# The last image's depthwise filter: the third channel tile on ScalarE and GpSimd, two sums in PSUM

## The chip, the cores and the metric

The kernel runs on one core of one Trainium2 chip. The metric is the device time of one execution in microseconds (us). The engines are named as in the profile: PE (TensorE, matrix products), PEld (its weight loads), DVE (VectorE), ACT (ScalarE), POOL (GpSimd) and SP (SyncE, which issues DMAs). Each engine runs its instructions in the order in which they were queued, and waits at an instruction whose inputs or buffers are not ready.

## The reference

The input `x` has 8 images of 384 channels and 64 x 64 points, all float32. Two layers follow each other. The first is `x + attention(group_norm(x))`, linear attention with six heads. The second, to which the change belongs, is

```python
t = jnp.einsum('bchw,oc->bohw', x, w_in)             # x is group-normalised
tp = t.reshape(b, hid, hb, P, wb, P)                 # 8 x 8 patches
tf = jnp.fft.rfft2(tp, axes=(3, 5))
tf = tf * fft_filter[None, :, None, :, None, :]
t = jnp.fft.irfft2(tf, s=(P, P), axes=(3, 5)).reshape(b, hid, h, w)
t = jax.lax.conv_general_dilated(t, w_dw, ..., feature_group_count=hid)   # 3 x 3, each channel alone
x1, x2 = (t[:, :hid // 2], t[:, hid // 2:])
g = jax.nn.gelu(x1, approximate=False) * x2
return jnp.einsum('bchw,oc->bohw', g, w_out)
```

and its result is added to the layer's input. The change moves part of the 3 x 3 filter, in which every channel has nine weights ("taps") of its own.

## The kernel before, in words

An image's 64 rows are cut into eight bands of 8 rows (512 points), and its 384 channels into three tiles of 128 partitions. The second layer takes one band at a time:

- `normalised` (L364 to L375): ACT writes the normalised band `hf`, three instructions.
- `expand_filter` (L745 to L774): PE makes `pi` in four quarters of 128 points, each a PSUM tile; ACT copies each to `ht`; PE turns `ht` into the patches' frequencies `pd`; DVE multiplies by the filter into `tf`.
- `back_transform` (L776 to L804): PE transforms back into `pb`; ACT copies that into a ring of two buffers that hold ten rows each, the band's eight and one edge row on either side. L801 copies the upper edge row from the band before, and L802 gives the band before its lower edge row. So a band's last three taps, which read its lower row, can run only once the next band is in the ring.
- `first_taps` (L839 to L846): ACT writes the first tap of each tile into the sums `dw`.
- `taps` and `tile_taps` (L848 to L860): DVE adds the other eight taps of each tile, one instruction each, `sum = ring * weight + sum` (L854), on 128 x 512 elements.
- `gate_taps` (L862 to L871): ACT takes the gelu of tile 0 (L866), and DVE multiplies it by tile 1 (L867). Tile 2 is gated with itself, half by half: two gelus on ACT (L870) and two products on DVE (L871). The result is `gated`.
- `contraction` (L877 to L917): PE multiplies `gated` by `w_out` into four PSUM tiles `pw`; ACT copies them to `y` (L912), and a DMA that POOL issues adds `y` to the output in memory (L917). For the very last band DVE adds instead (L914), and SP writes.

For the first seven images, the next image's first layer runs between these steps and fills PE. The last image has nothing to put between, and its second layer is a loop of its own at the end of the kernel (L1226 to L1246). In its last two bands PE filters the third tile with diagonal matrices (`on_array`, `array_taps`, PSUM tile `ptap`).

The order in which a scheduler queues the instructions on each engine is fixed when the kernel is built, by priority and by what each instruction needs. All PSUM tiles come from one pool of eight buffers, one per bank: `pi`, `pd`, `pb`, `pw` and `ptap` share them, and a tile waits for a buffer until the readers of its last holder are done. Work tiles in SBUF (`hf`, `ht`, `tf` and others) come from a pool of nine buffers (`w_tile`).

Of the kernel before, what the change touches and what calls it, by code (L numbers as in the profile page):

```python
# [9 lines left out]
F32 = mybir.dt.float32  # L10
BF16 = mybir.dt.bfloat16
AF = mybir.ActivationFunctionType
ALU = mybir.AluOpType

P = 128
C = 384
CT = 3
# [3 lines left out]
BT = N // NBAND  # L21
# [96 lines left out]
def conv_blocks_kernel(ctx: ExitStack, tc: tile.TileContext, a: dict, out: bass.AP, nb: int):  # L118
    nc = tc.nc
# [4 lines left out]
    taps_pool = ctx.enter_context(tc.tile_pool(name="taps", bufs=2))  # L124
# [5 lines left out]
    def ps_tile(name):  # L130
        return psum.tile([P, 512], F32, tag="ps", name=name)

    def w_tile(shape, name):
        return work.tile(shape, F32, tag="w", name=name)
# [98 lines left out]
    def const_tile(shape, name, src, queue=nc.scalar):  # L233
        t = const.tile(shape, F32, tag=name, name=name)
        queue.dma_start(t, src)
        return t
# [14 lines left out]
    scale = HD ** -0.5  # L251
# [9 lines left out]
    ring = []  # L261
# [543 lines left out]

    dw, dw_pe, diagonals = {}, {}, []

    def on_array(b, j):

        return b == nb - 1 and j >= NBAND - 2  # L810
# [7 lines left out]
    def array_taps(b, j, ks):  # L818

        for k in ks:  # L820
            nc.tensor.matmul(
                dw_pe[b, j].rearrange("p (r w) -> p r w", w=W),
                diagonals[0][:, k * P : (k + 1) * P],
                ring[j % 2][:, 2, k // 3 : k // 3 + 8, k % 3 : k % 3 + W],
                start=(k == 0),
                stop=(k == 8),
            )
# [3 lines left out]
    def add_tap(b, j, k, m0):  # L831

        t = w_tile([P, CT, 8, W], f"tap_{b}_{j}_{k}")
        for m in range(m0, CT):
            nc.scalar.activation(t[:, m], ring[j % 2][:, m, 0:8, k : k + W], AF.Copy, scale=w_dw[:, m, k : k + 1])
            first_on_vector[b, j, m] = k + 1
        nc.gpsimd.dma_start(out=dw[b, j][:, m0:], in_=t[:, m0:], accum_op=ALU.add)

    def first_taps(b, j):  # L839

        acc = dw[b, j] = taps_pool.tile([P, CT, 8, W], F32, tag="dw", name=f"dw_{b}_{j}")
        for m in range(CT - on_array(b, j)):
            nc.scalar.activation(acc[:, m], ring[j % 2][:, m, 0:8, 0:W], AF.Copy, scale=w_dw[:, m, 0:1])
        if on_array(b, j):
            dw_pe[b, j] = ps_tile(f"ptap_{b}_{j}")
            array_taps(b, j, range(9 if j == NBAND - 1 else 6))  # L846

    def tile_taps(b, j, m, weights, ks=None):  # L848

        t, acc = ring[j % 2], dw[b, j]  # L850
        for k in ks or range(first_on_vector.pop((b, j, m), 1), 9):
            src = t[:, m, k // 3 : k // 3 + 8, k % 3 : k % 3 + W]
            wd = weights[:, m, k : k + 1]
            nc.vector.scalar_tensor_tensor(acc[:, m], src, wd, acc[:, m], ALU.mult, ALU.add)  # L854

    def taps(b, j):
        if on_array(b, j) and j < NBAND - 1:
            array_taps(b, j, range(6, 9))
        for m in range(CT - on_array(b, j)):
            tile_taps(b, j, m, w_dw)  # L860

    def gate_taps(b, j):  # L862
        g = gated
        af = dw.pop((b, j)).rearrange("p t r w -> p t (r w)")
        last = dw_pe.pop((b, j)) if on_array(b, j) else af[:, 2, :]
        nc.scalar.activation(g[:, :BT], af[:, 0, :], AF.Gelu)  # L866
        nc.vector.tensor_mul(g[:, :BT], g[:, :BT], af[:, 1, :])  # L867
        for h, gelu in enumerate((gelu2[64:P, :], g[64:P, BT:])):
            of = slice(h * HT, (h + 1) * HT)
            nc.scalar.activation(gelu, last[0:64, of], AF.Gelu)  # L870
            nc.vector.tensor_mul(g[halves[h], BT:], gelu, last[64:P, of])  # L871

    def depthwise_gate(b, j):
        taps(b, j)
        gate_taps(b, j)
# [218 lines left out]
    for c0, at, n in QRUNS:  # L1094

        t, p0, quarter, first = at // P, at % P, c0 // QC, c0 % QC
# [13 lines left out]
    w_dw = const_tile([P, CT, 9], "w_dw", a["w_dw"], nc.sync)  # L1110
# [30 lines left out]
    def last_band(b):  # L1141

        for k in (1, 2):
            add_tap(b, NBAND - 1, k, 1)
            yield

        ps = ps_tile(f"pwd_{b}")
        nc.tensor.matmul(
            ps[:, : CT * 9], ident, w_dw.rearrange("p t k -> p (t k)"), start=True, stop=True
        )  # L1150
        late_w = small.tile([P, CT, 9], F32, tag="late_w", name=f"late_w_{b}", bufs=1)
        nc.vector.tensor_copy(late_w, ps[:, : CT * 9].rearrange("p (t k) -> p t k", t=CT))
        yield
        for m in range(CT):
            if m == 0:
                tile_taps(b, NBAND - 1, m, w_dw, range(1, 8))
                tile_taps(b, NBAND - 1, m, late_w, range(8, 9))
            else:
                tile_taps(b, NBAND - 1, m, late_w)
            if m == CT - 1:  # L1160
                gate_taps(b, NBAND - 1)
            yield
        if b + 1 < nb - 1:
            contract(b, NBAND - 1)

    before_last, late = nothing, iter(())
    for b in range(nb):
# [4 lines left out]
        last = b == nb - 1  # L1172
# [14 lines left out]
        for j in range(NBAND):  # L1187
# [19 lines left out]
            some(2 * items)  # L1207
            back_transform(b, j, tf[0])
            first_taps(b, j)
            some(items)  # L1210
            if j > 1:
# [15 lines left out]
    b = nb - 1  # L1227
    h = ahead
    for j in range(NBAND):
        tf = []  # L1230
        layer1 = expand_filter(b, j, h, tf)
        run(layer1)
        store_x(b, j)
        if j < NBAND - 1:
            h = normalised(b, j + 1, params, (8, 8), "f")
        back_transform(b, j, tf[0])
        first_taps(b, j)
        if j >= 2:
            contract(b, j - 2)
        if j >= 1:  # L1240
            taps(b, j - 1)
            gate_taps(b, j - 1)
    contract(b, NBAND - 2)
    taps(b, NBAND - 1)
    gate_taps(b, NBAND - 1)
    contract(b, NBAND - 1)  # L1246
# [41 lines left out]
```

## Time and profile before

| | us |
|---|---|
| median of 3 runs | 3333.89 |
| lowest and highest | 3331.0, 3337.78 |
| profiled execution, its own time | 3330.32 |
| span of the profiled execution, first to last instruction | 3328.5 |
| PE busy | 3264.3 |
| DVE busy | 2752.7 |
| ACT busy | 2024.5 |
| POOL busy | 173.3 |
| DVE taps (L854), 1401 of them | 976.6 |
| first instruction of the last stage (`hf` of band 0), from the span's start | 3150.11 |
| first `pi` product of the last stage | 3150.98 |

Times inside the profile are counted from the start of the span. In a row of the timeline, the columns are the start, the duration (of a whole group where it ends in "x3" and the like), the engine, the source line, the operation, output and inputs with shapes, the count, and in brackets how long the engine stood idle before it and what ended that. In a row of a group of instructions, the part after the bar has the busy time in us, the mean of one in ns, and the idle time before with what ended it.

### The profile page before, as it was taken

The numbers are of one execution on the slowest core, as the hardware profiler recorded it, in microseconds if no ns is written. First come the engines' busy times: TensorE is split into PE (matmuls) and PEld (weight loads), VectorE is DVE, ScalarE is ACT, GpSimd is POOL, SyncE is SP. The second block draws the span as 40 slices with busy tenths as digits, with TensorE's granted clock in tenths as the row PEclk, the third lists the DMA queues.
The fourth block names the chain that finished last, engine by engine and source line by source line (L and its number), as shares of the span: only waits on it lengthen the run. The fifth ranks groups of instructions, "written<-read, shape, count | busy, mean of one in ns | idle before, by whom it ended". The sixth has DMA issues, their size and how long they took to land.

```text
span 3328.5 us, 53155 instructions
## 1 busy us (share of the span) xinstructions
PE 3264.3 (98%) x21133; PEld 1830.2 (55%) x21133; DVE 2752.7 (83%) x4528; ACT 2024.5 (61%) x4029; POOL 173.3 (5%) x321
## 2 busy tenths in 40 slices
PE   8999999999999999999999999999999999999988
PEld 5544566456654566545665456654566445664454
DVE  6577789977889688896888968988788987989698
ACT  4445666556666566655666656656576665556553
POOL 0000000100010000100001000010000100000000
PEclk9999999999999999999999999999999999999999
DMA  6334335352444423534335343454333541324113
GB/s 217 113 93 110 96 80 128 112 143 68 108 108 123 143 66 97 127 100 141 86 82 134 115 122 77 104 133 114 103 96 96 134 134 42 86 71 127 57 25 53
DMA packets 154445, 346.33 MB, mean 104 GB/s; under 512 B 29812, under 2 KB 41060, under 8 KB 146004
## 3 DMA queue, kind: packets, MB, share of 16 engines
q1 hardware_dynamic: 124500, 282.65, 26.0%
q0 software_dynamic: 29504, 60.06, 12.2%
q8 instruction: 166, 2.72, 0.3%
q14 instruction: 83, 0.68, 0.1%
q10 hardware_dynamic: 192, 0.21, 0.0%
HBM read 235.62 MB, written 99.93 MB: 101 GB/s over the span
## 4 chain that ended last, share of the span: by engine, by line
PE 73%; DVE 14%; issue 6%; ACT 4%; DMA 2%; POOL 0%; SPq 0%; DVEq 0%; POOLq 0%; ACTq 0%
PE pk L491 14%; PE pi L751 14%; PE pv L507 13%; PE pf L733 11%; PE pq L654 6%; DVE dw L854 5%; PE pw L887 3%; PE pb L786 2%; PE pd L765 2%; PE acc L523 2%; PE pw L898 2%; PE acc L536 2%; DVE qc L666 1%; DVE qs L666 1%; DMA wq<-in_wq 1%
## 5 line engine op out<-in xcount | busy, mean ns | idle before, releaser
L854 DVE SCALAR_TENSOR_TENSOR dw<-ring,w_dw,dw 128x512 f32<-128x512 f32 x1401 | 976.6, 745 | 240.1 <-ACT ring L802 201.1
L491 PE MATMUL pk<-wk,x 128*128 128x384 f32 x1536 | 544.0, 495 | 0.0
L654 PE MATMUL pq<-x,wq 128*128 128x512 f32 x1152 | 528.3, 606 | 2.6 <-ACT mt L570 2.6
L751 PE MATMUL pi<-w_in,hf 128*128 128x384 f32 x1536 | 514.1, 492 | 1.3 <-ACT hf L374 1.3
L733 PE MATMUL pf<-qc,mt 128*128 128x512 f32 x1152 | 510.7, 597 | 1.2 <-ACT y L912 1.2
L507 PE MATMUL pv<-wv,x 128*128 128x384 f32 x1344 | 470.0, 488 | 0.0
L751 PEld LDWEIGHTS pi<-w_in,hf 128*128 128x128 f32 x1536 | 288.2, 191 | 196.1 <-issue 3.1
L491 PEld LDWEIGHTS pk<-wk,x 128*128 128x128 f32 x1536 | 283.1, 190 | 204.8 <-issue 31.6
L514 ACT COPY v<-pv 128x384 f32<-128x384 f32 x224 | 108.6, 485 | 424.7 <-PE pv L507 423.4
L733 PEld LDWEIGHTS pf<-qc,mt 128*128 128x128 f32 x1152 | 214.3, 190 | 256.8 <-issue 243.1
L507 PEld LDWEIGHTS pv<-wv,x 128*128 128x128 f32 x1344 | 253.6, 190 | 181.4 <-issue 8.4
L654 PEld LDWEIGHTS pq<-x,wq 128*128 128x128 f32 x1152 | 213.7, 192 | 249.1 <-issue 232.8
L737 DVE SCALAR_TENSOR_TENSOR x<-pf,bfc,x 128x512 f32<-128x512 f32 x192 | 137.7, 739 | 84.2 <-PE pf L733 84.1
L379 ACT ACTIVATE qs<-qc 128x512 f32<-128x512 f32 (+1 forms) x128 | 106.9, 836 | 163.9 <-DVE qc L683 163.9
L180 ACT ACTIVATE differences<-x,shift 128x512 f32<-128x512 f32 x168 | 120.1, 715 | 113.1 <-DVE x L737 112.9
L887 PE MATMUL pw<-gated,w_out 128*128 128x256 f32 x768 | 179.8, 384 | 0.0
L494 DVE TENSOR_TENSOR kc<-pk,kvbias 128x384 f32<-128x384 f32 x256 | 140.3, 548 | 38.7 <-PE pk L491 38.7
L758 ACT COPY ht<-pi 128x384 f32<-128x384 f32 x256 | 115.0, 482 | 86.2 <-PE pi L751 82.3
L887 PEld LDWEIGHTS pw<-gated,w_out 128*128 128x128 f32 x768 | 146.8, 192 | 37.0 <-issue 7.9
L917 POOL DMA_DIRECT2D out_dram<-y x63 | 80.5, 1278 | 1591.7 <-DVE dw L854 830.0
L379 ACT ACTIVATE ks<-kc 128x1536 f32<-128x1536 f32 x64 | 95.0, 1485 | 94.9 <-DVE kc L498 94.1
L374 ACT ACTIVATE hf<-x,nb,rs 128x512 f32<-128x512 f32 x192 | 146.3, 808 | 2.4 <-DVE nb L319 2.3
(209 smaller groups left out, 4375.4 us busy)
## 6 DMA issues: line engine op xcount, KB each, us to landing
tq<-in_tq SPq DMA_DIRECT2D x64, 1024.0 KB, 4.8
x<-in_x SPq DMA_DIRECT2D x64, 768.0 KB, 6.0
tk<-in_tk SPq DMA_DIRECT2D x64, 768.0 KB, 4.4
out_dram<-x SPq DMA_DIRECT2D x63, 768.0 KB, 3.5
out_dram<-y POOLq DMA_DIRECT2D x63, 768.0 KB, 7.7
xs<-in_x SPq DMA_DIRECT2D x56, 768.0 KB, 5.9
dw<-tap POOLq DMA_DIRECT2D x14, 512.0 KB, 9.5
wk<-in_wk SPq DMA_DIRECT2D x8, 576.0 KB, 3.9
```

What stands on the lines that cost most here:

```text
L180: nc.scalar.activation(out[:, m, :], x_[:, m, :], AF.Identity, bias=shift[:, m : m + 1], accum_out=of_m[0])
L374: nc.scalar.activation(dst, src, AF.Identity, bias=nb_[:, t : t + 1], scale=rs[:, t : t + 1])
L379: nc.scalar.activation(e, x_, AF.Relu, scale=-1.0)
L491: nc.tensor.matmul(pk[:, :C], tokens(t), wks[:, t, :], start=(t == 0), stop=(t == CT - 1))
L494: nc.vector.tensor_add(kc[:, i, :], pk[:, :C], bias)
L507: nc.tensor.matmul(pv[:, :C], xt[b, j][:, t, i * P : (i + 1) * P], wvs[:, t, :], start=(t == 0), stop=(t == CT - 1),)
L654: nc.tensor.matmul(p_, wqs[:, t, m * P : (m + 1) * P], xt[b, j][:, t, :], start=(t == 0), stop=(t == CT - 1),)
L733: nc.tensor.matmul(p_, mt[:, t, m * P : (m + 1) * P], q[:, t, :], start=(t == 0), stop=(t == CT - 1))
L737: latest["sum"] = nc.vector.scalar_tensor_tensor(xm, p_, bfc[:, m : m + 1], xm, ALU.add, ALU.add).ins
L751: nc.tensor.matmul(p_[:, :C], h[:, t, i * P : (i + 1) * P], w_in[:, t, :], start=(t == 0), stop=(t == CT - 1),)
L854: nc.vector.scalar_tensor_tensor(acc[:, m], src, wd, acc[:, m], ALU.mult, ALU.add)
L887: nc.tensor.matmul(p_[h][:, m - m0, :], w_out[:, 0, m * P : (m + 1) * P], gated[:, h * HT : (h + 1) * HT], start=(m == m0), stop=False,)
```

## The change

It applies to the last image alone (`alone(b)`).

- The sums of tiles 0 and 1 become PSUM tiles of their own (`dwp`), in all eight bands. ACT writes their first tap there, DVE adds the other eight taps there, and the gelu and the product of the gate read them there. The sum of tile 2 stays in SBUF.
- In the first six bands, tile 2 no longer goes through `tile_taps`. The new `apart_taps` has ACT write products `ring * weight` for taps 1 to 5, and POOL those for taps 6 to 8, three to a work tile. POOL then adds each product to the sum, in eight instructions.
- The last two bands keep the third tile on PE.

```diff
+    def alone(b):
+        return b == nb - 1
...
     def first_taps(b, j):
 
-        acc = dw[b, j] = taps_pool.tile([P, CT, 8, W], F32, tag="dw", name=f"dw_{b}_{j}")
+        whole = taps_pool.tile([P, CT, 8, W], F32, tag="dw", name=f"dw_{b}_{j}")
+        acc = [whole[:, m] for m in range(CT)]
+        if alone(b):
+            for m in range(2):
+                acc[m] = ps_tile(f"dwp_{b}_{j}_{m}").rearrange("p (r w) -> p r w", w=W)
+        dw[b, j] = whole, acc
         for m in range(CT - on_array(b, j)):
-            nc.scalar.activation(acc[:, m], ring[j % 2][:, m, 0:8, 0:W], AF.Copy, scale=w_dw[:, m, 0:1])
+            nc.scalar.activation(acc[m], ring[j % 2][:, m, 0:8, 0:W], AF.Copy, scale=w_dw[:, m, 0:1])
...
-            nc.vector.scalar_tensor_tensor(acc[:, m], src, wd, acc[:, m], ALU.mult, ALU.add)
+            nc.vector.scalar_tensor_tensor(acc, src, wd, acc, ALU.mult, ALU.add)
+
+    def apart_taps(b, j, m):
+
+        t, acc = ring[j % 2], dw[b, j][1][m]
+        for k in range(1, 9):
+            if k % 3 == 1:
+                products = w_tile([P, CT, 8, W], f"products_{b}_{j}_{k}")
+            product = products[:, (k - 1) % 3]
+            src = t[:, m, k // 3 : k // 3 + 8, k % 3 : k % 3 + W]
+            wd = w_dw[:, m, k : k + 1]
+            if k < 6:
+                nc.scalar.activation(product, src, AF.Copy, scale=wd)
+            else:
+                nc.gpsimd.tensor_scalar_mul(product, src, wd)
+            nc.gpsimd.tensor_add(acc, acc, product)
 
     def taps(b, j):
         if on_array(b, j) and j < NBAND - 1:
             array_taps(b, j, range(6, 9))
-        for m in range(CT - on_array(b, j)):
+        if alone(b) and not on_array(b, j):
+            apart_taps(b, j, 2)
+        for m in range(2 if alone(b) else CT):
             tile_taps(b, j, m, w_dw)
```

The gate reads the same sums from where they now lie.

More of the change, by code (lines that the diff above doesn't have):

```diff
@@ L836, in add_tap @@
             first_on_vector[b, j, m] = k + 1
-        nc.gpsimd.dma_start(out=dw[b, j][:, m0:], in_=t[:, m0:], accum_op=ALU.add)
+        nc.gpsimd.dma_start(out=dw[b, j][0][:, m0:], in_=t[:, m0:], accum_op=ALU.add)
     def first_taps(b, j):
-        acc = dw[b, j] = taps_pool.tile([P, CT, 8, W], F32, tag="dw", name=f"dw_{b}_{j}")
+        whole = taps_pool.tile([P, CT, 8, W], F32, tag="dw", name=f"dw_{b}_{j}")
[4 more added lines that the diff above has]
+        dw[b, j] = whole, acc
         for m in range(CT - on_array(b, j)):
-            nc.scalar.activation(acc[:, m], ring[j % 2][:, m, 0:8, 0:W], AF.Copy, scale=w_dw[:, m, 0:1])
+            nc.scalar.activation(acc[m], ring[j % 2][:, m, 0:8, 0:W], AF.Copy, scale=w_dw[:, m, 0:1])
         if on_array(b, j):
@@ L848, in tile_taps @@
     def tile_taps(b, j, m, weights, ks=None):
-        t, acc = ring[j % 2], dw[b, j]
+        t, acc = ring[j % 2], dw[b, j][1][m]
         for k in ks or range(first_on_vector.pop((b, j, m), 1), 9):
@@ L853, in tile_taps @@
             wd = weights[:, m, k : k + 1]
-            nc.vector.scalar_tensor_tensor(acc[:, m], src, wd, acc[:, m], ALU.mult, ALU.add)
+            nc.vector.scalar_tensor_tensor(acc, src, wd, acc, ALU.mult, ALU.add)
+    def apart_taps(b, j, m):
+        t, acc = ring[j % 2], dw[b, j][1][m]
+        for k in range(1, 9):
[9 more added lines that the diff above has]
+            nc.gpsimd.tensor_add(acc, acc, product)
     def taps(b, j):
@@ L863, in gate_taps @@
         g = gated
[L864 to L867, printed above, removed]
+        af = [t.rearrange("p r w -> p (r w)") for t in dw.pop((b, j))[1]]
+        last = dw_pe.pop((b, j)) if on_array(b, j) else af[2]
+        nc.scalar.activation(g[:, :BT], af[0], AF.Gelu)
+        nc.vector.tensor_mul(g[:, :BT], g[:, :BT], af[1])
         for h, gelu in enumerate((gelu2[64:P, :], g[64:P, BT:])):
```

## The prediction

> **What bounds the kernel now.** I read the page first. PE is busy 98% of the span at a granted clock of 0.992, so over most of the kernel VectorE (DVE) is hidden behind PE. GpSimd (POOL) does almost nothing.
>
> ```profile
> span 3328.5 us, 53155 instructions
> ...
> PE 3264.3 (98%) x21133; PEld 1830.2 (55%) x21133; DVE 2752.7 (83%) x4528; ACT 2024.5 (61%) x4029; POOL 173.3 (5%) x321
> ```
>
> The change touches only the last stage, so I read that stage next: busy time of each engine in windows from one `pi` group to the next, one window for each round of the loop over bands. Columns after the stretch are its length, then PE, PEld, DVE, ACT, POOL, the PE clock, the DMA share and GB/s.
>
> ```profile
> 3178.00:3197.00 19.00, 16.85 (x207) 10.87 (x198) 17.86 (x30) 15.10 (x34) 0.00 (x0) 1.00 0.01 2
> 3197.00:3218.00 21.00, 17.42 (x161) 10.94 (x161) 20.91 (x34) 10.01 (x25) 1.29 (x1) 0.92 0.26 38
> 3218.00:3238.00 20.00, 17.72 (x163) 11.72 (x162) 19.91 (x33) 12.25 (x29) 1.27 (x1) 0.91 0.27 41
> 3238.00:3258.00 20.00, 17.80 (x161) 11.18 (x161) 19.91 (x33) 10.57 (x25) 1.27 (x1) 0.91 0.27 41
> ```
>
> Here DVE is full (19.91 of 20 us), PE and ACT are not. The chain of waits in a steady stretch (3217 to 3260 us) agrees: nothing but DVE, four fifths of it taps.
>
> ```profile
> by line: DVE dw L854 79.7%; DVE tf L773 9.1%; issue 5.1%; DVE gated L871 3.9%; DVE gated L867 3.2%
> ```
>
> A round is counted from one `pi` group on PE to the next:
>
> ```profile
> 3237.74 8.01 PE L751 MATMUL pi<-w_in,hf 128*128 128x384 f32 x24
> ...
> 3257.69 8.01 PE L751 MATMUL pi<-w_in,hf 128*128 128x384 f32 x24
> ```
>
> From the group at 3178.64 us to the one at 3257.69 us there are four rounds, 19.8 us each. A tap takes 0.745 us and the next starts 0.67 us later (nine in 6.05 us). Nearer the end taps stand alone on one sum, and the chain shows them 0.79 us apart: waiting for one's own predecessor costs about 0.11 us.
>
> ```profile
> 3289.35 0.76 DVE dw L854
> 3290.14 0.76 DVE dw L854
> ```
>
> **What leaves and what comes.** Six bands lose the third tile's eight taps on DVE: 48 x 0.672 = 32.3 us. What remains there per band is 16 taps (10.8), four filter products (1.95) and the gate (1.5), 14.2 us. ACT gets five products per band; the nearest row is L843 (the first tap, the same form): 1.99 us for three, 0.66 each, 3.3 us per band, some 15 us a round in all with the 10 to 12 of the windows. GpSimd gets three products and eight adds per band, each add on the sum that the one before wrote. The final sum of tile 2 now comes from GpSimd, so the gelu of that tile on ACT (L870 before) waits for GpSimd. PE's work is unchanged.
>
> **The price of a GpSimd step.** No row of this trace is an add or a product on 512 elements there. Its groups of instructions by shape:
>
> ```profile
> L553 POOL COPY ks_bd<-key_sums 32x3 f32<-32x3 f32 x84 | 21.7, 259 | 56.6 <-DVE key_sums L622 53.2
> ...
> L446 POOL MEMSET xk<- 128x4 f32 x6 | 0.4, 112 | 62.9 <-DVE kc L381 62.9
> L257 POOL MEMSET kvt_bd<- 128x384 f32 x1 | 0.4, 418 | 0.3 <-POOLq L1278 0.3
> L259 POOL MEMSET ks_bd<- 128x96 f32 x1 | 0.2, 178 | 0.0
> ```
>
> The memsets give (418-178)/288 = 0.83 ns per element and 98 ns fixed; one stream of 512 elements is 0.525 us. That is the lower end for a step, with all streams side by side. An add moves three streams; one after the other they take 0.098 + 3 x 0.427 = 1.38 us. The copy of three elements takes 0.147 us more than a memset of four: fixed cost of an operation that reads. With 0.11 us for waiting on its predecessor an add is 1.64 us. With a fourth stream (a product also reads its factor from memory; how often, nothing shows) the upper end is 2.07 us. I take 1.6 us for either kind, by the three streams, the nearest count: 11 steps = 17.6 us per band. The ends are 5.8 and 22.8 us.
>
> The Trainium skill, GPSIMD Engine Reference, section 3.1, speaks against this change: it gives GpSimd about 2.6 cycles of 1.2 GHz per element for an add, 1.11 us on 512 (an estimate), and its section 4.1 says to leave elementwise work to VectorE, but calls one-input work roughly line-rate, 0.43 us (an estimate); eight and three of these with 0.11 us each for the hand-over are 11.4 us, and the sum below would end near 3340 us. No run here has shown either.
>
> **Who waits behind that.** ACT runs in order. The instruction order of the changed kernel puts this on ACT in a steady round: four `ht` copies of band j+1, three `hf` of band j+2, products 1 to 4 of band j, six ring copies, two edge rows and three first taps of band j+1, product 5 of band j, its gelu of tile 0, **its gelu of tile 2, which waits for GpSimd**, the four `y` copies of band j-1, the other gelu of band j, then the `ht` of band j+2. So behind the waiting gelu stand the `y` copies, and they hold PSUM: two sums of two bands are four of the eight banks, and `pw` has the other four. Quarter 0 of the next `pi` gets the bank that the gelu of tile 0 frees; quarters 1 to 3 get theirs only from the `y` copies. DVE stands still as well: its gate product of tile 2 is in order ahead of the next band's taps. PE thus waits for GpSimd, `ht` for PE, `hf` for ACT's order, and GpSimd's next band for the first product behind `hf`. All eleven GpSimd steps now lie on one loop.
>
> The ACT rows that price the loop, in a steady round of before:
>
> ```profile
> 3226.02 0.48 ACT L758 COPY ht<-pi 128x384 f32<-128x384 f32 x1 [1.46 <-PE pi L751]
> 3226.86 0.41 ACT L870 ACTIVATE gelu<-dw 64x256 f32<-64x256 f32 x1 [0.36 <-DVE dw L854]
> 3227.18 0.40 ACT L870 ACTIVATE gated<-dw 64x256 f32<-64x256 f32 x1
> 3227.61 2.22 ACT L374 ACTIVATE hf<-x,nb,rs 128x512 f32<-128x512 f32 x3
> ```
>
> From GpSimd's last add: gelu to the next issue 0.34, first `y` copy 0.56 (1.35 us for three, started 0.45 apart), three quarters of `pi` 6.0 (8.01 for four), `ht` 0.38, `hf` 2.12, first product 0.66, and four hand-overs between engines of about 0.06: 10.3 us. A round is 17.6 + 10.3 = 27.9 us.
>
> **The sum along that path.** GpSimd's first add for band 0 follows `hf` of band 2 (3173.72 + 2.22) and one product: 3176.6. Its eleven steps end at 3194.2. The first round is shorter, since `pi` finds free banks: only two gelus, three `ht`, `hf` and one product follow, 4.7 us, so 22.3 us: 3216.5. Four rounds of 27.9: 3328.1. Then, with the array's sum holding one more bank, gelu, `y` copy, two leftover `pw` matmuls (1.7 us) and the whole of the last `pi`. From that start to the last add before took 39.2 us (3282.88 to 3322.1), of PE work mostly; I keep it. The end is 3369.0 instead of 3322.1: +46.9 us. The profiled execution took 3330.32 us, so 3377 us. The median of the runs shown is 3.6 us above it; I stay with the profiled base.
>
> Costed at nothing: DVE's taps with a PSUM operand (L666 reads PSUM and takes the same 0.74 us; a PSUM output is in no row, and could be a tenth either way), covered by 27.9 - 14.2 = 13.7 us of idle DVE; without that cover 16 x 0.07 = 1.1 us a round. Products 2 to 4 push the ring copies back by about a microsecond, where ACT idled (2.66 us before L796): they sit beside GpSimd's adds. The `y` transfer's issue on GpSimd (1.27 us) falls into its idle 10 us. The order also shows one extra instruction on GpSimd, a load of its library ahead of the first add: it is reached at 3166.7, 9.9 us before that add is due; no row prices it, and I take 0 with an upper end of 10 us for a load twice its cover.
>
> The Trainium skill, GPSIMD Engine Reference, section 2.1, states some 6 us for such a load, which the cover would hide; no run here shows it.
>
> **The rivals.**
> GpSimd is cheap (steps near 0.525): its loop is 5.8 + 10.3 = 16.1 us and no longer decides. But quarter 0 of `pi` still waits for a bank that the gelu of tile 0 frees, behind `pi` 8.0, `ht` 0.5, `hf` 2.1, four products 2.6, ring and edge rows 2.1, six taps that need the edge row 4.1 and the gelu 0.6: 20.0 us, as long as the round now. DVE's relief is then eaten by PSUM: +2 to 3 us, 3333 us. It decides below a step of (20.0 - 10.3)/11 = 0.88 us. For it: DVE's own three-operand tap is only 0.745 us. Against: the copy row.
>
> Faster: DVE's relief reaches the end. With cheap steps (below 0.53) and banks that come free early enough, the round falls to PE's sum (8.01 + 1.52 + 1.63 + 2.75 + 1.57, and 0.6 of gaps) of 16.1 us: five rounds by 3.7 us, 3312 us. It needs `pi` not to wait for the tile-0 gelu; in the changed order its first matmul waits on an ACT count. Against it twice.
>
> Only the products are cheap (0.6 us, adds as taken): 14.6 us of steps, 6 x 3.0 = 18 us less, 3359 us. With adds near 1.2 as well, 3340 us.
>
> The library load outlasts its cover: up to 3387 us.
>
> **How the numbers follow.** The forecast's mechanism with steps of 1.4 to 1.85: 0.70; cheaper products or adds, still slower: 0.18; library late: 0.04; cheap GpSimd, no change: 0.06; faster: 0.02. Each 0.1 us of a step is worth 66 x 0.1 = 6.6 us. The range runs from steps of 1.07 (3342) to 1.85 (3394); outside it lie the cheap cases (0.08, and a little of the third rival) and dear steps. About 0.2%, 6.7 us, is what a measurement of this kernel can tell from no change. Faster 0.02, same 0.06, slower 0.92.
>
> **What would show it.** Right: in the stage's windows DVE falls to about half, POOL rises to 17 to 18 us of a 28 us round, ACT's gelu of tile 2 waits some 9 us on POOL, `pi` quarter 1 waits on `y`, and the time before 3165 us is as it was. Wrong: POOL adds well under 1.2 us, rounds near 20 us with PE waiting for the tile-0 gelu, or a wait of ACT on DVE taps.

## The result, and the profile after

The changed kernel takes 3375.0 us (median of 4 runs, 3373.28 to 3376.32); the kernel before takes 3333.97 us. The ratio is 1.0123, 95% interval 1.0108 to 1.0138: slower by 41 us. The forecast was 3377 us. What follows asks whether its reasons held as well as its number.

The page of the changed kernel, total and busy times:

```profile
span 3371.5 us, 53267 instructions
...
PE 3280.0 (97%) x21133; PEld 1835.0 (54%) x21133; DVE 2722.6 (81%) x4480; ACT 2043.2 (61%) x4059; POOL 261.8 (8%) x387
```

DVE lost 30 us of work, POOL gained 88, and the span grew by 43.0 us. Of these, 1.9 lie before the last stage (first `pi` at 3152.87 instead of 3150.98); the first `pi` of the experiments below starts anywhere from 3148.9 to 3154.8, so that part is scatter. From the first `pi` to the end of the last `x` add the stage takes 3364.87 - 3152.87 = 212.0 us, before it was 171.1: +40.9 us, all of the loss. Three steady rounds, in windows (columns as in the prediction):

```profile
3214.58:3241.97 27.39, 19.81 (x160) 12.11 (x160) 14.30 (x24) 14.12 (x31) 16.06 (x12) 0.82 0.20 30
3241.97:3269.55 27.58, 19.98 (x161) 12.18 (x161) 14.32 (x24) 14.13 (x31) 16.04 (x12) 0.81 0.20 30
3269.55:3296.98 27.43, 19.84 (x161) 12.21 (x161) 14.30 (x24) 14.12 (x31) 16.03 (x12) 0.81 0.20 30
```

A round is 27.5 us for 19.8. No engine is full: DVE is at 52%, POOL at 58%, and PE's clock fell from 0.91 to 0.82. So a loop of waits sets the round. One turn of it, from the chain of waits in order of time (start, duration, what; the steps of GpSimd between its first row and its last add are left out):

```profile
3253.25 0.58 POOL dw L877
...
3267.18 1.26 POOL dw L877
3268.49 0.42 issue
3268.91 0.59 ACT y L937
3269.50 0.04 issue
3269.55 7.82 PE pi L751 x18
3277.39 0.48 ACT ht L758
3277.87 2.12 ACT hf L374 x3
3279.99 0.62 ACT products L874
3280.62 0.08 issue
3280.69 0.58 POOL dw L877
```

GpSimd's eleven steps take 15.2 us. The 0.42 "issue" is the gelu of tile 2, which the chain steps over. Then the first `y` copy frees a bank, the last three quarters of `pi` follow (18 products, 7.8 us), `ht`, `hf`, the first product, and GpSimd's next band. The waits between 3214 and 3326 us name the same two places (total, times, longest), and PE's timeline shows quarter 0 running alone while quarters 1 to 3 wait for `y`:

```profile
ACT gelu L895 <- POOL dw L877: 31.2, 4, 9.5
...
PE pi L751 <- ACT y L937: 21.3, 4, 5.5
```

```profile
3234.26 2.20 PE L751 MATMUL pi<-w_in,hf 128*128 128x384 f32 x6
3241.97 7.94 PE L751 MATMUL pi<-w_in,hf 128*128 128x384 f32 x18 [5.51 <-ACT y L937]
```

Groups of GpSimd's instructions give what no row of before had:

```profile
L877 POOL TENSOR_TENSOR dw<-dw,products 128x512 f32<-128x512 f32 x48 | 60.7, 1264 | 51.2 <-ACT products L874 48.4
...
L876 POOL TENSOR_SCALAR products<-ring,w_dw 128x512 f32<-128x512 f32 x18 | 27.9, 1556 | 0.0
```

An add is 1.26 us (1.34 from one to the next), a product 1.56.

### The profile page after: what moved, and what is told of

The parts are those of the page before. It is cut to its first block, busy times and chain, and to the rows that moved or that the text cites. A ratio compares the mean times of both kernels' runs of the same rounds, so it can differ in the third digit from the quotient of the medians.

```text
span 3371.5 us, 53267 instructions
## 1 busy us (share of the span) xinstructions
PE 3280.0 (97%) x21133; PEld 1835.0 (54%) x21133; DVE 2722.6 (81%) x4480; ACT 2043.2 (61%) x4059; POOL 261.8 (8%) x387
## 3 DMA queue, kind: packets, MB, share of 16 engines
q1 hardware_dynamic: 124500, 282.65, 25.7%
## 4 chain that ended last, share of the span: by engine, by line
PE 67%; issue 12%; DVE 9%; DMA 4%; ACT 3%; POOL 3%; SPq 0%; DVEq 0%; POOLq 0%; ACTq 0%
PE pi L751 15%; PE pk L491 14%; PE pv L507 13%; PE pf L733 7%; PE pw L912 3%; PE pq L654 3%; PE pd L765 2%; PE pb L786 2%; DVE dw L862 2%; PE acc L523 2%; PE acc L536 2%; DMA wq<-in_wq 2%; PE pw L923 2%; POOL dw L877 2%; DMA inverse<-of_groups 1%
## 5 line engine op out<-in xcount | busy, mean ns | idle before, releaser
L862 DVE SCALAR_TENSOR_TENSOR dw<-ring,w_dw,dw 128x512 f32<-128x512 f32 x1225 | 858.6, 746 | 231.8 <-ACT ring L802 196.4
L751 PE MATMUL pi<-w_in,hf 128*128 128x384 f32 x1536 | 523.5, 498 | 25.6 <-ACT y L937 21.3
L773 DVE TENSOR_TENSOR tf<-pd,filt 128x384 f32<-128x384 f32 x256 | 127.3, 549 | 37.9 <-PE pd L765 37.8
```

What stands on the lines that cost most here:

```text
L751: nc.tensor.matmul(p_[:, :C], h[:, t, i * P : (i + 1) * P], w_in[:, t, :], start=(t == 0), stop=(t == CT - 1),)
L773: nc.vector.tensor_mul(tf[:, 2 * s + i, :], p_[i][:, :C], filt)
L862: nc.vector.scalar_tensor_tensor(acc, src, wd, acc, ALU.mult, ALU.add)
```

## The experiments

Theory A is the prediction's: the last stage waits for GpSimd's chain, because ScalarE stands in order at the gelu of tile 2, and behind it stand the `y` copies that hold PSUM. Rival B: the two sums in PSUM are the cost, whatever GpSimd does. Rival C: GpSimd's work hinders the other engines by itself. Each kernel is compared with the kernel before on its own chip. "Stage" is the time from the first `pi` to the end of the last `x` add, less the 171.1 us of before; the last column is the time from one band's `pi` to the next in the steady part.

| kernel | median us | before us | difference | ratio (95%) | stage | round us |
|---|---|---|---|---|---|---|
| changed | 3375.0 | 3333.97 | +41.0 | 1.0123 (1.0108 to 1.0138) | +40.9 | 27.5 |
| psum_only | 3339.69 | 3331.2 | +8.5 | 1.0026 (1.0015 to 1.0036) | +9.8 | 20.2 to 20.8 |
| apart_sbuf | 3367.09 | 3331.2 | +35.9 | 1.0110 (1.0095 to 1.0125) | +37.1 | 24.6 to 32.8 |
| act_products | 3338.3 | 3331.2 | +7.1 | 1.0022 (1.0013 to 1.0032) | +7.2 | 20.05 |
| warm | 3364.89 | 3331.2 | +33.7 | 1.0101 (1.0086 to 1.0116) | +34.1 | 25.7 |
| y_dve | 3360.04 | 3330.22 | +29.8 | 1.0087 (1.0072 to 1.0102) | +28.5 | 23.3 |
| no_wait | 3331.39 | 3330.22 | +1.2 | 1.0002 (0.9992 to 1.0011) | +0.9 | 19.4 |
| no_wait_sbuf | 3354.83 | 3330.22 | +24.6 | 1.0073 (1.0058 to 1.0088) | +27.0 | 24.3 to 27.7 |
| dma1 | 3332.18 | 3330.22 | +2.0 | 1.0002 (0.9993 to 1.0012) | -0.2 | 19.7 |
| gate_pool | 3374.78 | 3333.33 | +41.5 | 1.0126 (1.0109 to 1.0143) | +42.4 | 27.6 |
| y_gate | 3350.13 | 3333.33 | +16.8 | 1.0050 (1.0035 to 1.0065) | +15.5 | 20.5 |

**psum_only: only the sums move.**

```diff
-        if alone(b) and not on_array(b, j):
-            apart_taps(b, j, 2)
-        for m in range(2 if alone(b) else CT):
+        for m in range(CT - on_array(b, j)):
             tile_taps(b, j, m, w_dw)
```

> The sums of tiles 0 and 1 stay in PSUM; the third tile goes back to DVE, so GpSimd filters nothing. Theory A (the chain of eleven GpSimd steps is what the last stage waits for): nearly all of the 41 us goes. DVE is full again with 19.8 us of work a round; what PSUM may still cost is that quarter 0 of pi waits for the bank of the gelu of tile 0, a round of 20.0 to 20.8 us: 3334 to 3341 us. Rival B (the sums in PSUM are the cost, by the banks they hold): half of the loss or more stays, 3355 to 3375 us, with PE waiting for y copies as in the changed kernel.

Measured +8.5 us, rounds of 20.2 to 20.8. B falls as the main cause, but a fifth of the loss stays where the sums alone move. `pi` now waits up to 1.73 us a round for the bank that the gelu of tile 0 frees, but this wait is not where most of the 9.8 us are lost. The fourth band's `pi` starts 52.0 us after the first, 45.9 before, so 6.1 us are lost while the loop fills; there the third `pi` takes 10.78 us and waits for the ring copies, which free the banks of `pb`. The next three rounds together take 61.7 us, 60.8 before, and VectorE is full in them (a window of psum_only):

```profile
3224.69:3245.46 20.77, 16.23 (x160) 10.19 (x160) 20.64 (x34) 10.98 (x26) 1.27 (x1) 1.00 0.26 40
```

A tap into PSUM takes 0.750 us (median of 128 in the changed kernel) against 0.745 (176 in the stage of before): the taps themselves cost nothing.

**apart_sbuf: only the third tile moves.**

```diff
-        if alone(b):
-            for m in range(2):
-                acc[m] = ps_tile(f"dwp_{b}_{j}_{m}").rearrange("p (r w) -> p r w", w=W)
```

> The third tile stays on ScalarE and GpSimd; all sums lie in SBUF again. Theory A with the banks as its second half: the eleven steps (15.2 us in the changed kernel's trace) and ScalarE's wait in the gelu stay, but pi finds its banks during the wait, so the 7.8 us of pi and the 0.6 us of the first y copy leave the loop, and the left-over ht copies (about 1.2) and perhaps the issue of the y transfer (1.3) enter it: a round of 21 to 22 us for 27.4, so 3375 - 5 x 5.9 = 3345 us, between 3340 and 3351. Theory A without banks (the GpSimd chain alone): 3370 to 3375. Rival B (PSUM is all of it): 3327 to 3336 us. If VectorE and GpSimd hinder each other where both read SBUF alone, GpSimd's add grows from 1.26 us, or the tap from 0.746.

A miss: +35.9 us where A had about 11. The instructions of the stage that touch the sums show why (minimum, median, maximum in ns). First apart_sbuf, then the same adds with the sums in PSUM:

```profile
L859 DVE SCALAR_TENSOR_TENSOR dw<-ring,w_dw,dw x128: 737/747/2681, 3168.4 to 3350.1; 128x512 f32<-128x512 f32 x128
L874 POOL TENSOR_TENSOR dw<-dw,products x48: 1260/1592/1792, 3177.5 to 3321.1; 128x512 f32<-128x512 f32 x48
...
L889 DVE TENSOR_TENSOR gated<-gated,dw x8: 680/1745/1751, 3190.8 to 3353.4; 128x512 f32<-128x512 f32 x8
```

```profile
L877 POOL TENSOR_TENSOR dw<-dw,products x48: 1253/1263/1277, 3178.3 to 3322.0; 128x512 f32<-128x512 f32 x48
```

With the sums in SBUF, VectorE and GpSimd hinder each other. The add goes from 1.26 to 1.59 us (median), GpSimd's product from 1.56 to 1.88 (means), single taps from 0.75 up to 2.68, the gate product from 0.68 to 1.75. The place of the two sums is all that was edited, so the move to PSUM has a purpose that the prediction did not see: it keeps the two engines apart. The Trainium skill, "SBUF — State Buffer", section "Who interferes with whom", states this: a VectorE instruction with two SBUF inputs contends with a GpSimd instruction that reads SBUF, one with at most one, outside the two-port modes that the page names, does not. Both halves agree with these rows: a tap with its sum in SBUF takes 2.68 us at most, one with its sum in PSUM 0.757.

**act_products: three products less on GpSimd.**

```diff
-            if k < 6:
+            if k < 9:
                 nc.scalar.activation(product, src, AF.Copy, scale=wd)
```

> Products 6 to 8 move from GpSimd to ScalarE; GpSimd keeps the eight adds. Theory A: its chain shortens by three products at 1.55 us, 4.65 us a round, to 10.7; ScalarE makes the three in the time in which it waited. Round 27.4 - 4.65 = 22.8 us, six bands x 4.65 = 28 us less: 3347 us. If PE's shorter wait also lets the clock stay at 1.00, 1.8 us a round more: 3339 us. Rival B (banks held by the sums decide, whatever GpSimd does): 3370 to 3375 us. Rival C (ScalarE is the bound, and three more products of 0.62 lie on its path): no better than 3365 us.

Measured +7.1 us, the lower of A's two numbers. The round fell by 7.4 us to 20.05, more than the three products are worth, and GpSimd is no longer in the chain at all. Chain by line from 3215 to 3260 us, and the wait that takes over:

```profile
by line: PE pi L751 35.7%; ACT products L874 21.9%; ACT ring L796 11.5%; ACT hf L374 9.4%; ACT dwp L851 8.0%; ACT dw L851 4.2%; issue 3.9%; ACT ring L802 2.6%; ACT gated L891 2.2%; ACT ht L758 2.1%; ACT ring L801 0.4%; ACTq L937 0.1%
```

```profile
3243.26 8.01 PE L751 MATMUL pi<-w_in,hf 128*128 128x384 f32 x24 [1.74 <-ACT gated L891]
3263.30 8.01 PE L751 MATMUL pi<-w_in,hf 128*128 128x384 f32 x24 [1.74 <-ACT gated L891]
```

PE's clock is 1.00 all through these rounds. This is the loop of the prediction's first rival: all of `pi` waits for the bank that the gelu of tile 0 (L891) frees. But a round of 20.05 us is no longer than one of before; of the 7.2 us that the stage loses, 5.8 are lost by the fourth band's `pi` (51.7 us after the first, 45.9 before).

**warm: PE kept busy during the wait.** Quarter 0 of `pi` is computed three times over.

```diff
-            for t in range(CT):
+            for t in (*range(CT),) * (3 if alone(b) and 3 <= j <= 6 and i == 0 else 1):
```

> In bands 3 to 6 of the last image PE computes quarter 0 of pi three times over, which fills 4.0 of the 5 us in which it stood idle ahead of quarters 1 to 3. Theory A with the clock: these quarters took 7.8 us for 18 products instead of 6.0 because the granted clock was 0.5 for their first 3.6 us after the idle time; with PE busy the clock stays at 1.00, and each of the four rounds loses 1.8 us: 3375 - 7.2 = 3368 us, with quarters 1 to 3 in 6.0 us. Rival (the quarters are slow because the y copies release their banks one by one, 0.45 us apart): no change, 3375 us, quarters still 7.8 us. If the repeated quarter gets in the way of the loop: up to 4 x 4 = 16 us more.

Measured +33.7 us, 7.3 less than the changed kernel, and the quarters are at full speed:

```profile
3239.11 6.07 PE L751 MATMUL pi<-w_in,hf 128*128 128x384 f32 x18 [2.18 <-ACT y L937]
3264.82 6.07 PE L751 MATMUL pi<-w_in,hf 128*128 128x384 f32 x18 [1.64 <-ACT y L937]
```

In the changed kernel, PE alone in short windows (length, busy, clock, DMA share, GB/s), after 4.80 us of idle time:

```profile
3212.00:3214.50 2.50, 0.00 (x0) 1.00 0.00 0
3214.58:3216.58 2.00, 2.00 (x4) 0.62 0.00 0
3216.58:3218.58 2.00, 2.00 (x4) 0.53 0.51 44
3218.58:3220.58 2.00, 2.00 (x8) 1.00 1.00 142
```

For some 4 us PE starts four products in 2 us, and eight in the 2 us after. In warm the clock is 1.00 through quarters 1 to 3, although `pi` still waits for `y`, so the rival (banks released one by one) falls. Twelve products that are thrown away shorten each of the four rounds by 1.8 us. So a wait of PE costs here more than its own length.

**y_dve: the banks of `pw` no longer wait behind ScalarE.**

```diff
-                    nc.scalar.copy(y[of], p_[h][:, : m1 - m0, :])
+                    (nc.vector.tensor_copy if alone(b) else nc.scalar.copy)(y[of], p_[h][:, : m1 - m0, :])
```

> The changed kernel, but in the last image VectorE, which stands idle half of the time, copies pw to y instead of ScalarE, so that the banks of pw no longer wait behind ScalarE's gelu of tile 2. The sums stay in PSUM and the third tile on GpSimd. Theory A with banks: quarters 1 to 3 of pi run during GpSimd's chain, and the loop becomes the eleven steps 15.2, gelu 0.5, three ht copies 1.2, hf 2.1, product 0.7, perhaps the issue of the y transfer 1.3: 19.7 to 21 us for 27.4. Where VectorE's own order holds a y copy back, part of it stays. 13 to 26 us above the kernel before (the changed one stands 41 above it). Rival (the banks are only where PE waits, not what the loop costs): no better than 35 above.

Measured +29.8 us, rounds of 23.3: better than the changed kernel by 11 us, but a miss, since 13 to 26 us were expected. `pi` no longer waits for `y`, but the chain now goes another way, through VectorE:

```profile
3237.97 0.43 ACT gelu L895
3238.39 0.02 issue
3238.42 0.42 DVE gated L896
3238.84 0.03 issue
3238.87 0.43 DVE gated L896
3239.32 5.38 DVE dwp L862 x8
3244.70 0.02 issue
3244.72 0.76 DVE dwp L862
3245.48 0.03 issue
3245.51 0.57 DVE tf L773
```

After it come the back transform, the ring copies, the edge row, and only then GpSimd's products, which read that row. VectorE stands in order at tile 2's gate product, so nine taps and the filter product start late.

**gate_pool and y_gate: VectorE waits for GpSimd nowhere.** gate_pool has this edit alone, y_gate has it and y_dve's:

```diff
-            nc.vector.tensor_mul(g[halves[h], BT:], gelu, last[64:P, of])
+            (nc.gpsimd if alone(b) and not on_array(b, j) else nc.vector).tensor_mul(g[halves[h], BT:], gelu, last[64:P, of])
```

> The changed kernel with the two gate products of tile 2 on GpSimd instead of VectorE in the first six bands, so that VectorE waits for GpSimd nowhere. It is there to see what VectorE's standing still costs by itself. Theory A: nothing, since the loop runs through ScalarE's gelu, the y copies and pi, not through VectorE: 38 to 44 us above the kernel before, as the changed kernel. Rival (VectorE's wait at the gate product is part of the loop, as in y_dve's chain, where nine taps of 6.1 us follow it): 3 us a round less, 25 to 30 above.

> Both: VectorE copies pw to y, and GpSimd makes the two gate products of tile 2. Neither the banks of pw nor VectorE's taps and filter products then wait for GpSimd; only ScalarE's gelu of tile 2, and behind it ht and hf, do. Theory A after y_dve's chain (gelu, gate products, nine taps, filter products, back transform, ring copies, edge row, and only then GpSimd's products): with VectorE out of it the loop is the eleven steps 15.2, gelu 0.5, three ht 1.2, hf 2.1, product 0.7 and some 1 to 1.5 us for the gate products and the y issue on GpSimd: 20 to 21 us for 23.3 in y_dve, so 13 to 20 us above the kernel before instead of 30. If y_dve's 23.3 us are due to the chain's length alone: no better than 27 above.

Measured +41.5 and +16.8 us, as A has it. VectorE's wait costs nothing in the changed kernel, where the banks are later anyway; with the banks free it costs 13 us. The waits lie one behind another, and taking away one brings out the next.

**no_wait and no_wait_sbuf: nobody waits for GpSimd.** The second also has apart_sbuf's edit.

```diff
-            nc.gpsimd.tensor_add(acc, acc, product)
+            nc.gpsimd.tensor_add(product, product, product)
```

> GpSimd and ScalarE do all their work on the third tile, but GpSimd adds each product to itself instead of to the sum, so that the gelu of tile 2 waits for nobody (the output lacks eight taps of the third tile in six bands). Theory A: the wait was the loss; what stays is the loop of the bank that the gelu of tile 0 frees, as in act_products (20.05 us there, with three products more on ScalarE): rounds of 19.5 to 20.0 us, 2 to 8 us above the kernel before. Rival (GpSimd's work slows the others by itself, whoever waits for it): over 15 us above.

> As no_wait (the output lacks the same taps), and the sums of tiles 0 and 1 lie in SBUF: no wait for GpSimd and no bank held. Without contention between VectorE and GpSimd nothing is left but PE's sum of 16 to 17.7 us a round: 8 to 12 us below the kernel before. With the contention that apart_sbuf's rows suggest (a tap beside a GpSimd step takes 1.66 us instead of 0.67, a GpSimd step 1.6 to 1.8): eleven steps 18 us, in which VectorE does 11 of its 16 taps; the other five 3.4, the filter products 2.0 and the gate 1.5 make 23 to 25 us a round: 15 to 25 us above the kernel before, with no engine waiting for GpSimd.

Measured +1.2 and +24.6 us: the first just under A's 2 to 8, the second within its 15 to 25, though its rounds are longer than the 23 to 25 us named. In no_wait GpSimd still does 66 arithmetic steps (its adds read one tile twice and take 1.05 us in the mean), and no loss can be measured: rival C falls for sums in PSUM, and the wait is the loss. In no_wait_sbuf nobody waits for GpSimd and no sum holds a bank, and 25 us are lost. One round of each, no_wait first:

```profile
3239.77:3259.17 19.40, 16.23 (x160) 10.18 (x160) 15.57 (x24) 14.04 (x31) 14.16 (x13) 1.00 0.28 42
```

```profile
3253.89:3280.12 26.23, 17.87 (x163) 11.97 (x161) 22.32 (x25) 14.48 (x32) 18.16 (x13) 0.80 0.21 31
```

For about as many instructions VectorE needs 22.3 us instead of 15.6, and GpSimd 18.2 instead of 14.2, so the contention is seen in both engines. A little of it is in no_wait too: tile 2's gate products, with both inputs in SBUF, now run beside GpSimd and take 0.69 and 0.93 us (means of the stage) instead of 0.42, but VectorE has time to spare there.

**dma1: two taps of the kernel before as products that a DMA adds.** Made from the kernel before.

```diff
         first_taps(b, j)
+        if not on_array(b, j):
+            add_tap(b, j, 1, 1)
```

> The kernel before, but in the last image's first six bands ScalarE writes the second tap of tiles 1 and 2 as products and a DMA adds them to the sums, as the earlier images' last bands do. VectorE loses two taps a band, 1.34 us, with no bank held and no GpSimd arithmetic. If VectorE is the bound as read: rounds of 18.5 for 19.8 us, 3 to 8 us below the kernel before. If the transfer (9.5 us to landing for 512 KB in the trace) is late for the taps behind it, or ScalarE's two products push the ring copies back: no change to 6 us above.

A miss: no change that can be measured. VectorE loses two taps a band, and the rounds stay at 19.7 us. VectorE is as full in them as before, with 33 instructions a round in both; before, then dma1:

```profile
3217.97:3237.74 19.77, 17.49 (x163) 11.49 (x161) 19.68 (x33) 12.02 (x28) 1.27 (x1) 0.91 0.28 42
```

```profile
3216.78:3236.50 19.72, 17.68 (x162) 11.51 (x160) 19.62 (x33) 13.63 (x31) 2.20 (x2) 0.91 0.41 68
```

The windows of the tail, again before and then dma1, show where the taps went:

```profile
3283.00:3326.00 43.00, 35.00 (x232) 21.14 (x232) 30.78 (x51) 13.22 (x34) 4.07 (x4) 0.96 0.41 69
```

```profile
3283.00:3326.00 43.00, 33.26 (x228) 20.06 (x226) 25.10 (x42) 11.33 (x28) 3.81 (x4) 0.95 0.43 74
```

VectorE used the time to work ahead, with 42 instead of 51 instructions left at the end, where it is not the bound. So a full VectorE in the windows of before did not mean that fewer taps end earlier. Whether the order of VectorE's instructions, fixed when the kernel is built, keeps the round at 19.7 us was not tested.

None of these kernels is measurably faster than the kernel before.

## Why the prediction was right

**The mechanism held.** The chain shows the predicted loop step by step, and `pi` splits at quarter 1, as forecast. no_wait shows that the wait is the loss, act_products that GpSimd's length sets it, y_dve and y_gate that the order on ScalarE and VectorE and the banks behind it carry it on. No run changes the order on ScalarE itself.

**Two terms were mis-sized, and one took back half of the other.** A GpSimd step was taken at 1.6 us, by counting streams. Adds measured 1.34 with the hand-over and products 1.55, so a chain is 15.22 us for 17.6, and six chains are 14.3 us less than forecast. The count of streams gave both kinds one price, but the product, which reads one tile and a factor per partition, is dearer than the add, which reads two tiles. The way back was taken at 10.3 us; it is 12.2. Nearly all of that is `pi`: three quarters at 6.0 us were priced at the full clock, and they took 7.8, since PE had stood still. Over four rounds that is 7.6 us more. With the start 0.2 us early and the tail 0.7 us longer (41.6 for 40.9), the stage comes to 46.9 - 14.3 + 7.6 - 0.2 + 0.7 = 40.7 us, and 40.9 were measured. So the loss was forecast 6 us too large, 46.9 us for 41.0. That 3377 lies only 2 us from the measured 3375.0 is in part luck: the forecast was added to the profiled execution, 3330.32 us, which is 3.7 us under the median of before. The signs named for it fit with these sizes: DVE at 14.3 of 27.5 us, POOL at 16.0 (14.7 and the issue of a DMA) where 17 to 18 were named, and ACT idle for 7.2 us ahead of the gelu of tile 2, not 9.

**What was costed at nothing.** PSUM operands cost nothing (a tap 0.750 us for 0.745). The library load does not show: the first add starts 0.08 us after its product, as in every later round. The time before 3165 us is 1.9 us later, within the scatter named above.

**What the sum left out.** It held no contention between VectorE and GpSimd, and none shows in the changed kernel (taps 0.757 us at most, adds 1.277), but only because the change puts the sums into PSUM. The prediction treated the PSUM sums as a cost of banks alone.

**The rivals.** The cheap GpSimd was priced at a 20.0 us round and +2 to 3 us. Where GpSimd no longer decides, the round is 20.05 (act_products) and 19.4 us (no_wait), the end +7.1 and +1.2 us: the wait that it named is there, and no version run here with the sums in PSUM has a round under 19.4 us. Its +2 to 3 us are not shown to come from that round, since most of what act_products loses is lost before the fourth band. The faster case has no support: with nobody waiting for GpSimd (no_wait) nothing is gained (though that case's condition was not met: `pi` still waits 1.08 us for the tile-0 gelu), and dma1 weakens its premise, that relief of VectorE reaches the end. The cheap products (0.6 us) are refuted at 1.56. There row and page differ: by the Trainium skill's GPSIMD Engine Reference, section 4.1, one-input work is roughly line-rate, 0.43 us on 512 elements (an estimate), where the product measured 1.56; its section 3.1 would make an add 1.11 us (an estimate), near the measured 1.26.

## What to carry to other kernels

Before work is moved to an idle but slower engine, find who waits for its last step, and follow what is queued in order behind that wait on each waiting engine, down to the buffers that this work would have freed. Price a wait of PE with the slow products after it. And look at which memory both engines read: here neither place for the sums was free, since SBUF cost contention (25 us with nobody waiting) and PSUM cost 8.5 us when the sums alone moved, most of it while the loop fills.

## What the runs showed of the hardware that was not expected

- After PE stood idle for about 5 us the granted clock was 0.53 to 0.62 for some 4 us; with 4.0 of the 5 us filled by spare products it was 1.00 for the products that follow, and 18 of them took 6.07 instead of 7.8 us.
- With two SBUF inputs a tap on VectorE beside a GpSimd step took up to 2.68 us instead of 0.75, and GpSimd's add 1.59 instead of 1.26; with the sum in PSUM both were undisturbed (0.757 and 1.277 us at most).
- A GpSimd product with one streamed input (1.56 us) is dearer than its two-input add (1.26 us), and an add that reads one tile twice takes 1.05 us (mean).
